# Reordering the turn of a period in layer 0: transposes ahead of the output's first tile, its evacuation behind 13 taps

## The chip, the cores and the metric

The kernel runs on one core of a Trainium2 chip. The metric is the time of the whole kernel on the device in microseconds (us), as the median of several runs; lower is better. Durations of single instructions come from one profiled execution.

## What is computed

The input x has two images of 512 channels and 64 x 64 pixels, in float32. Two layers follow, each added to its input; the change concerns the first only.

```
# layer 0: x = x + L0(group_norm(x))
xproj  = inp @ in_w + in_b                         # 512 -> 512, per pixel
x1     = gelu(layer_norm(depthwise_3x3(inp) + dw_b))
offset = x1 @ off_w + off_b                        # 16 groups x 9 points x 2
mask   = softmax((x1 @ mask_w + mask_b) over the 9 points)
out    = dcnv3(xproj, offset, mask)                # bilinear samples of xproj, weighted by the mask
L0     = out @ out_w + out_b
# layer 1: x = x + relu(batch_norm(fc(px + softmax(scores(px)) @ v(px)))) on group_norm(x)
```

## The kernel before

Layer 0 takes the first third of the time (to about 1275 us). Each image is cut into 8 chunks of 512 pixels (8 rows of 64), so there are 16 chunks. The bilinear samples of a pixel lie in a window of 5 x 5 pixels; the kernel turns offsets and mask into 25 weights for each pixel and group, and sampling becomes a matmul of a small weight matrix with a patch of xproj. The work on a chunk has four stages, each a Python generator whose `yield`s mark steps:

- `project(i)`, 13 steps: read the raw rows (`raw`, L737); four ACT instructions that normalize them to `xn` (L748); then four times a matmul `pq` (L758) and an ACT copy to `xj` (L764) with two stores to `xt` in HBM (L766).
- `features(i)`, 39 steps: four ACT instructions that seed `conv` with one tap of the depthwise kernel (L783); 32 DVE instructions for the other taps (L788), with sums `tot` on POOL (L794, L796); a matmul for the mean (L801), the subtraction (L806), squares (L809), a matmul for the variance, root (L818), reciprocal and product (L820, L821), and Gelu in two steps (L825).
- `weights(i)`, 27 steps: four times a matmul `po` (L842) and a DVE add into `o` (L847); exp, hats and softmax on ACT and DVE; nine steps with products `pk` (L885) added to `aw` (L890); one ACT copy of `aw` to `at` (L893); then four times four transposes (`p_tr`, L901) with an ACT copy to `awT` (L902).
- `sample(i)`: eight times four matmuls `pb` (L930) and a copy to `bt` (L935); eight times eight matmuls `pa` (L949) of a patch with `bt` and four copies of 32 partitions each to `dT` (L960), with reads of `res` (L941) and the fetch of the next chunk's half patch after the last of a half (`fetch`, eight DMAs, L914); then four output tiles, each a matmul `py` (L969), and in a step of its own the addition of the residual on DVE (L974), its statistics (L975) and a store `wx` (L976).

A fifth generator, `image_stats(1)`, has 64 steps; each loads one piece `xraw` of the second image (L711), two steps ahead of its use, and takes `bn_stats` of an earlier one on DVE (L713). Period 5 begins by running what is left of it, the group norm's small steps.

A loop over the 16 chunks calls `period` once for each. In it, `m` is the sampling of chunk i, `y` the rest of the sampling of chunk i - 1 (its output tiles), `v` the rest of the weights of chunk i (the transposes), `w` the weights of chunk i + 1 up to `at`, `f` the features of chunk i + 2, `g` the first step (seeds) of those of chunk i + 3, `p` the projection of chunk i + 3, and `more` a step of the statistics. `m(2)` means two steps of `m`. Chains of chunks beyond the last are empty, as is `y` in period 0.

The order of these calls is written out by hand and fixes the order of instructions on every engine and queue, since the loop runs under `tc.manual_schedule()`; each engine executes its own list in that order and waits by semaphores. All DMAs of this stage are issued from SP's queue, in the same order. PSUM has four banks under the tag "mm" (`pq`, `po`, `p_tr`, `py` and the means) and two double ones under "big" (`pb`, `pa`). `xj`, `dT` and `patch` have two buffers each, `raw` and `xraw` three, `res` four; `conv`, `at` and `aw` have one.

Of the kernel before, what the change touches and what calls it, by code (L numbers as in the profile page):

```python
# [570 lines left out]
def window_path(ctx: ExitStack, tc: tile.TileContext, t_in: dict, out: bass.AP, far: bass.AP, sums: bass.AP):  # L571
# [58 lines left out]
    with ExitStack() as l0:  # L630
# [66 lines left out]
        def image_stats(n):  # L697

            mv = sm.tile([P, KB, 2], F32, name="gn_mv")
            size = CH if n == 0 else CH // 2  # L700
            pieces, ahead = deque((kb, h) for kb in range(KB) for h in range(S // size)), deque()
            for kb in range(KB):
                st = sm.tile([P, 16, 6], F32, name="gn_st")
                for h in range(S // size):
                    if n == 0:
                        t = img[kb][:, h * size : (h + 1) * size]
                    else:
                        while len(ahead) < 3 and pieces:
                            k2, h2 = pieces.popleft()
                            ahead.append(io.tile([P, size], F32, name="xraw", bufs=3))  # L710
                            nc.sync.dma_start(ahead[-1], x_v[n, :, k2, h2 * size : (h2 + 1) * size])  # L711
                        t = ahead.popleft()
                    nc.vector.bn_stats(st[:, h, :], t)  # L713
                    yield
                nc.vector.bn_aggr(mv[:, kb, :], st[:, : S // size].rearrange("p a b -> p (a b)"))
            yield
            result = []
            yield from group_norm_steps(mv, KB, sm, ps, result)
            sc, bi = result
            gn[n] = [sm.tile([P, KB], F32, name=f"gn_{k}{n}") for k in ("scale", "bias")]  # L720
            nc.vector.tensor_copy(gn[n][0], sc)
            nc.vector.tensor_copy(gn[n][1], bi)
# [184 lines left out]
        def fetch(i, s):  # L907

            if i >= NSEQ:
                return  # L910
            n, ch = divmod(i, NCH)
            t = io.tile([P, PX, C], F32, name="patch", bufs=2)
            for p in range(PX):
                nc.sync.dma_start(  # L914
                    t[:SN, p, :], xt_d[n][ch * ROWS + PR * s : ch * ROWS + PR * s + SY, PC * p : PC * p + SX, :]
                )
            patches[i, s] = t

        def sample(i):

            n, ch = divmod(i, NCH)
            at = [awT[32 * t : 32 * t + NW].rearrange("w g (c s r p) -> w c r g s p", c=2, s=2, r=PR) for t in range(4)]

            for d0 in range(0, PR * PC, 4):
                pb = ps.tile([P, 4, 2 * PX * G], F32, tag="big", bufs=2, name="pb")

                for k in (0, 2, 1, 3):
                    r, c = divmod(d0 + k, PC)
                    off, t = SEL0 - (r * SX + c), c // 2
                    nc.tensor.matmul(  # L930
                        pb[:SN, k, :], sel[32 * t : 32 * t + NW, off : off + SN], at[t][:, c % 2, r], start=True, stop=True
                    )

                copy = nc.vector.tensor_copy if i == NSEQ - 1 and d0 % PC else nc.scalar.copy
                copy(bt[:SN].rearrange("s g q d -> s d (g q)")[:, d0 : d0 + 4, :], pb[:SN])  # L935
                yield
            res = {}

            def read(cb):
                res[cb] = io.tile([P, CH], F32, name="res", bufs=4)  # L940
                nc.sync.dma_start(res[cb], x_v[n, :, cb, ch * CH : (ch + 1) * CH])  # L941

            dT = cv.tile([P, KB, CH], F32, tag="dT", name="dT", bufs=2)
            for s in range(2):
                xp = patches.pop((i, s))
                for cb in range(KB):
                    pa = ps.tile([P, PX, 4, PR * PC], F32, tag="big", bufs=2, name="pa")
                    for p in range(PX):
                        nc.tensor.matmul(  # L949
                            pa[:, p], xp[:SN, p, cb * P : (cb + 1) * P],  # L950
                            bt[:SN, 4 * cb : 4 * cb + 4, PX * s + p, :], start=True, stop=True,
                        )

                    for q in range(4):
                        rows = slice(CG * q, CG * (q + 1))
                        dst = dT[rows, cb, s * (CH // 2) : (s + 1) * (CH // 2)].rearrange(
                            "p (r q c) -> p q r c", r=PR, c=PC)
                        src = pa[rows, :, q, :].rearrange("p q (r c) -> p q r c", c=PC)
                        copy = nc.vector.tensor_copy if i == NSEQ - 1 and q % 2 else nc.scalar.copy
                        copy(dst, src)  # L960
                    if s:
                        read(cb)
                    if cb == KB - 1:
                        fetch(i + 1, s)
                    yield
            for cb in range(KB):
                py = ps.tile([P, CH], F32, tag="mm", name="py")
                for kb in range(KB):
                    nc.tensor.matmul(  # L969
                        py, out_w[:, kb, cb * P : (cb + 1) * P], dT[:, kb, :], start=(kb == 0), stop=(kb == KB - 1)  # L970
                    )
                yield
                t = res.pop(cb)
                nc.vector.scalar_tensor_tensor(t, py, out_b[:, cb : cb + 1], t, ALU.add, ALU.add)  # L974
                nc.vector.bn_stats(stats2[n][:, cb, ch, :], t)  # L975
                nc.sync.dma_start(x1_d[n][ch][:, cb, :], t)  # L976
                yield
# [20 lines left out]
        def period(y, v, m, w, f, g, p, more):  # L998

            p()
            y()
            v(4)
            f(4)
            y()
            for taps in (9, 7, 6, 6):
                m(2)
                w()  # L1010
                more()
                f(taps)
                w()
                more()
            w()
            m()
            w()
            m()
            f()
            y()  # L1020
            f()
            m()
            p()
            w(2)
            y(2)
            w()
            m()
            p()
            f()
            w(2)  # L1030
            p()
            y(2)
            f()
            y()
            m()
            p()
            more()
            for k, steps in enumerate((1, 2, 2, 2)):
                p()
                w(steps)  # L1040
                if k == 0:
                    f()
                p()
                more()
                if k < 3:
                    m()
                if k == 0:
                    f()
                if k == 2:
                    g()  # L1050
            w()

        def value_weights():

# [26 lines left out]
        v = Chain(weights, 0)  # L1081
        v(23)
        run(features(1), project(2), output_bias())
        fetch(0, 0)
        fetch(0, 1)
        later, y, f = image_stats(1), Chain(sample, NSEQ), Chain(features, 2)
        with tc.manual_schedule():
            f()
            for i in range(NSEQ):
                if i == NCH - 3:  # L1090
                    run(later)
                w, m, g = Chain(weights, i + 1), Chain(sample, i), Chain(features, i + 3)
                period(y, v, m, w, f, g, Chain(project, i + 3), lambda: next(later, None))
                y, v, f = m, w, g
            y.rest()
# [5 lines left out]
    with ExitStack() as l1, tc.manual_schedule():  # L1101
# [8 lines left out]
        with ExitStack() as at, ExitStack() as inner:  # L1110
# [177 lines left out]
            for n in range(NB):  # L1288
# [9 lines left out]
                for i in range(NCH // 2):  # L1298
                    if 0 < i < 3 or n and i == 0:
                        k = i + 1 if i else 1  # L1300
# [26 lines left out]
                for qb in range(NCH):  # L1327
                    acc = {}
                    for kp in range(NPAIR + 2):
# [23 lines left out]
                        if kp < NPAIR:  # L1353
                            v = ready.pop(0)
                            e, tt, _ = made[qb, kp]
                            ops = operands(lambda k: e[:, k, :], tt)
                        else:
                            v = w7[:, kp - NPAIR]
# [174 lines left out]
```

## Time and profile before

| What | us |
|---|---|
| median of 3 runs (3700.46 to 3703.06) | 3702.26 |
| the profiled execution, its own time | 3707.44 |
| its span | 3705.6 |
| PE busy with matmuls | 3417.9 (92%) |
| DVE busy | 2345.8 (63%) |
| ACT busy | 1304.1 (35%) |
| POOL busy | 291.0 (8%) |
| a period from turn 1 to turn 5 | 72.9 to 75.9 |
| a period from turn 7 to turn 13 | 67.6 to 67.7 |
| period 14 | 56.9 |

The busy times of PE are modelled from pipelined matmuls, so 92% does not mean 92% of its peak. A matmul in float32 leaves two records in the trace. The shares of the page are averages over two layers with different limits; the change is confined to the periods of layer 0, whose length is the distance from one `p_tr` to the next.

In a line of the timeline the columns are start, duration, engine, line of the kernel, operation, output<-inputs, shapes and count; in brackets stand the idle time of the engine ahead of it and what ended that. In the chain of waits they are start, duration and what was at work; "SPq" is SP's queue that issues DMAs.

### The profile page before, as it was taken

The numbers are of one execution on the slowest core, as the hardware profiler recorded it, in microseconds if no ns is written. First come the engines' busy times: TensorE is split into PE (matmuls) and PEld (weight loads), VectorE is DVE, ScalarE is ACT, GpSimd is POOL, SyncE is SP. The second block draws the span as 40 slices with busy tenths as digits, with TensorE's granted clock in tenths as the row PEclk, the third lists the DMA queues.
The fourth block names the chain that finished last, engine by engine and source line by source line (L and its number), as shares of the span: only waits on it lengthen the run. The fifth ranks groups of instructions, "written<-read, shape, count | busy, mean of one in ns | idle before, by whom it ended". The sixth has DMA issues, their size and how long they took to land.

```text
span 3705.6 us, 39010 instructions
## 1 busy us (share of the span) xinstructions
PE 3417.9 (92%) x15151; PEld 2433.8 (66%) x15151; DVE 2345.8 (63%) x3575; ACT 1304.1 (35%) x1691; POOL 291.0 (8%) x190
## 2 busy tenths in 40 slices
PE   4689998999998799999999999999999999999990
PEld 1355555555555477777777777777777777777770
DVE  5798989999996475545554554567455455545544
ACT  2476777787886321111111111221111111111114
POOL 2112111212111030000000000022000000000000
PEclk9789999999999899999999999999999999999995
DMA  7233442342432444334334333444433333243349
GB/s 240 63 98 114 135 137 83 115 133 83 127 109 78 142 157 171 126 129 139 123 108 163 122 125 130 140 155 169 149 121 111 122 138 111 101 149 121 111 162 389
DMA packets 180181, 500.06 MB, mean 135 GB/s; under 512 B 22640, under 2 KB 64368, under 8 KB 170512
## 3 DMA queue, kind: packets, MB, share of 16 engines
q1 hardware_dynamic: 176496, 473.34, 37.5%
q10 hardware_dynamic: 3456, 24.12, 1.7%
q8 instruction: 121, 1.98, 0.2%
q14 instruction: 76, 0.62, 0.0%
q0 software_dynamic: 32, 0.00, 0.0%
HBM read 406.09 MB, written 91.29 MB: 134 GB/s over the span
## 4 chain that ended last, share of the span: by engine, by line
PE 75%; DVE 15%; DMA 4%; ACT 2%; SPq 1%; issue 1%; POOL 1%; ACTq 0%; DVEq 0%; POOLq 0%
PE acc L1364 41%; DVE conv L788 8%; PE pS L1211 7%; PE p L1402 7%; PE py L969 5%; PE pq L758 4%; PE pa L949 4%; PE pv L1251 3%; PE pk L1305 1%; PE p_mean L801 1%; DVE pk L885 1%; DVE aw L890 1%; DMA patch<-xt 1%; DMA out<-ct 1%; DVE o L847 1%
## 5 line engine op out<-in xcount | busy, mean ns | idle before, releaser
L1364 PE MATMUL acc<-e,v 128*128 128x256 f32 x3072 | 768.2, 386 | 0.0
L1215 ACT ACTIVATE e<-pS 128x1024 f32<-128x1024 f32 x256 | 262.0, 1024 | 1386.4 <-PE pS L1211 1313.0
L1364 PE MATMUL acc<-tt,v 128*128 128x256 f32 x3072 | 748.2, 380 | 0.5 <-DMA v<-wv 0.5
L1364 PEld LDWEIGHTS acc<-e,v 128*128 128x128 f32 x3072 | 566.5, 190 | 233.2 <-issue 165.3
L1364 PEld LDWEIGHTS acc<-tt,v 128*128 128x128 f32 x3072 | 582.4, 190 | 91.2 <-issue 10.6
L1218 DVE TENSOR_TENSOR t<-e 128x256 f32<-128x256 f32 x256 | 108.8, 425 | 761.1 <-ACT e L1215 761.1
L788 DVE SCALAR_TENSOR_TENSOR conv<-xn,L_conv_dw_w_sb,conv 128x504 f32<-128x504 f32 (+1 forms) x512 | 399.7, 795 | 48.5 <-ACT conv L783 36.5
L1228 DVE TENSOR_TENSOR tot<-tot,e 128x512 f32<-128x512 f32 x480 | 330.1, 688 | 8.3
L949 PEld LDWEIGHTS pa<-bt,patch 96*128 96x128 f32 x2048 | 251.8, 197 | 63.1 <-issue 39.4
L1211 PE MATMUL pS<-q,kq 64*128 64x512 f32 x1024 | 289.0, 641 | 0.0
L949 PE MATMUL pa<-bt,patch 96*128 96x128 f32 x2048 | 255.3, 281 | 9.3 <-ACT dT L960 5.8
L935 ACT COPY bt<-pb 96x1024 f32<-96x1024 f32 x124 | 234.2, 2001 | 58.9 <-PE pb L930 58.9
L758 PE MATMUL pq<-L_conv_in_w_sb,xn 128*128 128x512 f32 x512 | 236.3, 605 | 4.3 <-ACT xn L748 4.3
L969 PE MATMUL py<-dT,L_conv_out_w_sb 128*128 128x512 f32 x512 | 238.0, 610 | 0.0
L1402 PE MATMUL p<-t,v 128*128 128x256 f32 x1024 | 231.4, 382 | 1.7 <-DMA v<-wv 1.7
L1402 PEld LDWEIGHTS p<-t,v 128*128 128x128 f32 x1024 | 192.1, 190 | 48.5 <-issue 21.2
L960 ACT COPY dT<-pa 32x256 f32<-32x256 f32 x496 | 179.5, 362 | 89.8 <-PE pa L949 80.9
L842 PE MATMUL po<-om_w_pg,feat 128*128 128x432 f32 x512 | 203.4, 542 | 0.0
L969 PEld LDWEIGHTS py<-dT,L_conv_out_w_sb 128*128 128x128 f32 x512 | 99.3, 197 | 119.6 <-issue 115.5
L758 PEld LDWEIGHTS pq<-L_conv_in_w_sb,xn 128*128 128x128 f32 x512 | 94.1, 194 | 109.5 <-issue 93.0
L842 PEld LDWEIGHTS po<-om_w_pg,feat 128*128 128x128 f32 x512 | 93.0, 191 | 90.5 <-issue 89.4
L1211 PEld LDWEIGHTS pS<-q,kq 64*128 64x128 f32 x1024 | 77.1, 184 | 84.9 <-issue 84.9
(203 smaller groups left out, 3731.2 us busy)
## 6 DMA issues: line engine op xcount, KB each, us to landing
v<-wv SPq DMA_DIRECT2D x252, 768.0 KB
patch<-xt SPq DMA_DIRECT2D x256, 192.0 KB
v<-wv SPq DMA_DIRECT2D x256, 128.0 KB
wv<-v SPq DMA_DIRECT2D x32, 896.0 KB
xt<-xj SPq DMA_DIRECT2D x128, 128.0 KB
res<-in_x SPq DMA_DIRECT2D x64, 256.0 KB
wx<-res SPq DMA_DIRECT2D x64, 256.0 KB
xq<-wx SPq DMA_DIRECT2D x16, 1024.0 KB
```

Source lines behind the costliest of these rows:

```text
L758: nc.tensor.matmul(pq, xn[:, kb, 1 + 2 * t : 3 + 2 * t, :].rearrange("p r c -> p (r c)"), in_w[:, kb, :], start=(kb == 0), stop=(kb == KB ...
L788: nc.vector.scalar_tensor_tensor(dst, src, wt, dst, ALU.mult, ALU.add)
L842: nc.tensor.matmul(po[:, : 3 * GP], f[:, kb, t * P : (t + 1) * P], om_w[:, kb].rearrange("p a k g -> p (a k g)"), start=(kb == 0), stop=(k ...
L935: copy(bt[:SN].rearrange("s g q d -> s d (g q)")[:, d0 : d0 + 4, :], pb[:SN])
L949: nc.tensor.matmul(pa[:, p], xp[:SN, p, cb * P : (cb + 1) * P], bt[:SN, 4 * cb : 4 * cb + 4, PX * s + p, :], start=True, stop=True,)
L960: copy(dst, src)
L969: nc.tensor.matmul(py, out_w[:, kb, cb * P : (cb + 1) * P], dT[:, kb, :], start=(kb == 0), stop=(kb == KB - 1))
L1211: nc.tensor.matmul(pS[:, h, :], kq[r, 2 * (kp // 4) + h, c0 : c0 + P], qs[qb][r, :], start=True, stop=True)
L1215: nc.scalar.activation(e.rearrange("p a q -> p (a q)"), pS.rearrange("p h q -> p (h q)"), AF.Exp)
L1228: nc.vector.tensor_add(tots[qb], tots[qb], e2[:, h, :])
L1364: nc.tensor.matmul(acc[j][:, cb * HQ : (cb + 1) * HQ], v[:, j, cb * P : (cb + 1) * P], ops[j], start=(kp + cb == 0), stop=(kp + cb == NPAI ...
L1402: nc.tensor.matmul(p7[:, cb * HQ : (cb + 1) * HQ], v7[:, cb * P : (cb + 1) * P], t3, start=(k + cb == 0), stop=(k + cb == NPAIR + 2),)
```

## The change

`sample` gets one more `yield`, between the eight matmuls `pa` and their copies to `dT`, so that they can be called separately. In `period`, `m()` becomes `m(2)` where `pa` is meant, and the last copies of the half (with the read of `res` and the fetch) become the last step of the period, behind the fourth `pq`, `at` and the fourth `xj`. The call `g()` moves from behind the last `pa` to ahead of the second `xj`. `at` joins the last products in `w(3)`. At the start of the next period `v(4)` (transposes) goes ahead of `y()` (the first `py`), and the second `y()` (its residual, statistics and store) from behind four taps to behind the first `f(taps)`, so behind 13.

```diff
--- before.py
+++ after.py
@@ -950,6 +950,7 @@
                             pa[:, p], xp[:SN, p, cb * P : (cb + 1) * P],
                             bt[:SN, 4 * cb : 4 * cb + 4, PX * s + p, :], start=True, stop=True,
                         )
+                    yield
 
                     for q in range(4):
                         rows = slice(CG * q, CG * (q + 1))
@@ -1001,30 +1002,31 @@
 
 
             p()
+            v(4)
             y()
-            v(4)
             f(4)
-            y()
-            for taps in (9, 7, 6, 6):
+            for k, taps in enumerate((9, 7, 6, 6)):
                 m(2)
                 w()
                 more()
                 f(taps)
+                if k == 0:
+                    y()
                 w()
                 more()
             w()
-            m()
+            m(2)
             w()
-            m()
+            m(2)
             f()
             y()
             f()
-            m()
+            m(2)
             p()
             w(2)
             y(2)
             w()
-            m()
+            m(2)
             p()
             f()
             w(2)
@@ -1032,23 +1034,32 @@
             y(2)
             f()
             y()
+            m(2)
+            p()
+            more()
+            p()
+            w()
+            f()
+            p()
+            more()
+            m(2)
+            f()
+            p()
+            w(2)
+            g()
+            p()
+            more()
+            m(2)
+            p()
+            w(2)
+            p()
+            more()
             m()
             p()
+            w(3)
+            p()
             more()
-            for k, steps in enumerate((1, 2, 2, 2)):
-                p()
-                w(steps)
-                if k == 0:
-                    f()
-                p()
-                more()
-                if k < 3:
-                    m()
-                if k == 0:
-                    f()
-                if k == 2:
-                    g()
-            w()
+            m()
 
         def value_weights():
```

## The prediction

> **What bounds the kernel now.** I call the start of a period its turn, and number turns by the period that begins there. The transposes start turns 1 to 15 at 244.15, 319.48, 395.39, 470.11, 542.97, 619.77, 687.47, 755.18, 822.88, 890.57, 958.28, 1025.98, 1093.62, 1156.94 and 1213.85 us. Everything outside the periods is untouched, so I read only them. First the busy time of each engine in one ordinary period (turn 8 to turn 9):
>
> ```profile
> 755.18:822.88 67.70, 64.44 (x309) 38.34 (x309) 62.67 (x72) 53.77 (x72) 12.98 (x9) 1.00 0.36 112
> ```
>
> The columns are length, then PE, weight load, DVE, ACT and POOL. PE has 3.3 us free, DVE 5.0, ACT 13.9: no engine has much room, so order decides. Next the waits of DVE in that period, then the timeline of its turn:
>
> ```profile
> DVE conv L788 <- ACT conv L783: 1.8, 1, 1.8
> DVE res L974 <- PE py L969: 1.4, 1, 1.4
> ```
>
> ```profile
> 747.03 0.76 DVE L890 TENSOR_TENSOR aw<-aw,pk 128x576 f32<-128x576 f32 x1
> 748.75 2.93 ACT L783 ACTIVATE conv<-xn,L_conv_dw_b_sb,L_conv_dw_w_sb 128x512 f32<-128x512 f32 x4
> ...
> 752.19 2.93 ACT L893 COPY at<-aw 128x1600 f32<-128x1600 f32 x1
> 754.12 0.75 DVE L974 SCALAR_TENSOR_TENSOR res<-py,L_conv_out_b_sb,res 128x512 f32<-128x512 f32 x1 [1.42 <-PE py L969]
> 755.18 1.97 PE L901 MATMUL p_tr<-ident,at 128*128 128x128 f32 x16 [1.10 <-ACT at L893]
> 755.87 2.05 ACT L902 COPY awT<-p_tr 128x512 f32<-128x512 f32 x4 [0.75 <-PE p_tr L901]
> 757.98 1.14 PE L930 MATMUL pb<-awT,sel 25*96 25x256 f32 x16 [0.83 <-ACT awT L902]
> 762.28 0.60 DVE L847 TENSOR_TENSOR o<-po,om_b_pg 128x432 f32<-128x432 f32 x1
> ```
>
> The two DVE waits (the fourth tile's seeds; the output's first tile py0) are its only ones there, 3.24 us. Yet a second path ends at the same instant. ACT works through Gelus, seeds and the copy `at`; PE transposes; ACT copies awT; PE runs pb and the first po; and po ends at 762.21 (759.04 + 3.17), just ahead of DVE's first `o` add at 762.28. So removing the DVE waits alone buys nothing: that add waits for po. From it on DVE is unbroken up to the tap that starts the mean, and the period's length follows.
>
> In turns 1 to 4, the second image's statistics are read as well. There the chain of waits goes through the SP queue (turn 3):
>
> ```profile
> 389.33 0.46 SPq L941
> ...
> 394.89 6.70 DMA patch<-xt
> 401.59 0.02 issue
> 401.61 4.18 DMA xraw<-in_x
> 405.79 0.03 issue
> 405.81 0.43 DVE gn_st L713
> ```
>
> The eight patch DMAs issue from 389.89; SP holds one xraw load until the eighth patch lands; the load takes 4.18 us; DVE, which needs it before its next seven taps, stands still for 2.05 us (1.62, 2.87, 2.05 and 1.34 in turns 1 to 4).
>
> **What the Trainium skill says.** "DMA: Bandwidth & Descriptors", section "Queues, rings and completion order": on each DMA engine descriptors are consumed in ring order. So a load queued behind patches and raws lands after them; the trace agrees (4.18 us here, 2.39 for an xraw load at 234.35 with no patches ahead). "TensorE: Matmul & The Clock Gate", Part 1: idle for about 3.4 us, PE falls to half clock and needs about as long busy to return. The trace agrees: after 5.8 us idle 16 pa records took 3.78 us against 1.95. "Perfetto Trace Analysis", "Optimization Strategy": equal gaps that repeat can mean too few buffers; PE's 1.10 at the transposes is no such gap (it ends with ACT's `at`), but the change makes one, below.
>
> **The change, part by part.** No instruction is added or removed; the new yield only splits pa from its evacuation, and all but the last of the eight are still taken in pairs. Moves:
>
> (a) ACT: the seeds go from behind the last dT copies to ahead of xj1; `at` and xj3 go ahead of the last dT copies. Same work. In before, the Gelu table load starts at 735.51 and xj2's slot ends at 746.42 without a gap: 10.91. Add the seeds' slot, 2.96 (748.75 to 751.71): `at` starts 749.38 (its input was ready at 747.79) and ends 752.31, 2.81 earlier than now. Then xj3 0.48 and dT 1.51: the first awT copy starts at 754.27, ends 754.86.
>
> (b) PE: transposes at 752.37, done by 754.3. Then py0, now between them and pb. py0 needs one of the four "mm" banks. They rotate: in turn 5 the fourth transpose waited 0.53 for the first awT copy, being in its bank. With four transposes ahead, py0 is the one that gets that bank: it starts at 754.9, not 754.3. 3.45 for py0 and 0.1 to start: pb at 758.45 against 757.98; the `o` add 4.30 later, 762.75 against 762.28. **+0.4** a turn (I shade +0.47 for the 0.08 by which DVE, not po, was last). Without the bank wait it is -0.15; with the ACT copies landing later than their slots, +1.0. Both ends stay: -0.2 to +1.0. Eight ordinary turns (6 to 13): **+3.2** (-1.6 to +8).
>
> (c) DVE: res0 goes behind 13 taps. From 747.8 thirteen taps take 10.1, to 757.9; res0 waits for py0 until 758.4 and ends 759.8; the add waits until 762.75. DVE's idle moves from 3.24 in two places to some 3 us in one. Queued behind it: the remaining 19 taps, exactly what sets the end. The wx store of res0 follows later; nobody near needs it.
>
> (d) SP: res3's read and the eight patches move from ahead of xj3's two stores and an xraw load to behind them; the raws stay behind the patches. In ordinary turns, cost nothing: the patches serve pa some 35 us later, raws serve xn as late. In turns 1 to 4 it costs. By (a) in turn 3, `at` starts at 389.6, xj3 at 392.5; stores, load and read (1.14 + 0.53 + 0.46 and gaps) let the patches begin at 395.4, not 389.89; the other three turns give 6.0. In its place the load gets ahead of some things: the eighth DMA before it is now the fourth patch (in before it is the eighth patch, and that is the landing it waited for), and the store of res0 is behind it. So SP issues it at some 403.5, not 401.61. Landing: before, 1.9 MB from the first patch to 401.59, less 2 us to start, is 198 GB/s; eight patches of 192 KB then take 7.8 + 2 from 395.4, to 405.2; three raws and the load (1.09 MB at the 385 GB/s of that stretch) 2.8 and 0.7 to finish: 408.7 against 405.79. **+2.9**, and I take 3.0. Lower end 0.7 (it lands 3 us after issue), upper 5.9 (whole shift). DVE reaches this load at 404.6, so it decides. The xraw load behind xj1 comes 3 us later too, and holds DVE until 391.4 ahead of its four taps; the add is then at 403.7 and the load still decides. Four turns: **+12** (3 to 23). Turn 0 has no output before it: nothing.
>
> (e) Turn 5 (group norm's steps in between): DVE is last; its taps start 0.6 sooner, res0 is the same work: **-0.4**.
>
> (f) Turns 14 and 15 have no seeds or taps: PE waits for `at`, which waits for DVE.
>
> ```profile
> 1156.94 2.42 PE L901 MATMUL p_tr<-ident,at 128*128 128x128 f32 x16 [2.33 <-ACT at L893]
> 1160.03 2.05 PE L930 MATMUL pb<-awT,sel 25*96 25x256 f32 x16 [0.68 <-ACT awT L902]
> ```
>
> py0, now done in that idle time, goes between transposes and pb. PE is then idle 6.2 us and cold: transposes 3.7 (as at 1213.85), py0 4.3, pb at 1164.9; warm by then, pb and po save 2.4 of their cold 6.75. **+2.5** there, and at turn 15, where a warmed PE makes pb cheaper, **+1.5**. Together 4 (0 to 9).
>
> Sum: 3.2 + 12 - 0.4 + 4 = 18.8. The profiled execution took 3707.44 (span 3705.6), so 3726.2 under the profiler; it lies 5.18 above the median, which I carry over: 3702.26 + 18.8 = **3721**.
>
> **Rivals.** *Patches late in full*: every turn of 1 to 4 pays the 5.9: 3702.3 + 23.6 + 3.2 + 3.6 = 3733. For it: the chain runs through the patches. Against: the load is no longer behind the eighth. 22%. *Loads covered*: statistics turns cost 0.7 and the tail's clock makes good py0: 3702.3 + 2.8 + 3 = 3708. For it: raws and patches share engines, so landing could compress. 17%. *DVE's waits are the bound*: the 3.24 of eight turns and 5.25, 4.85, 4.03, 2.76 of turns 1 to 4 all go, 42.8: 3659. It decides if po ends before DVE's 759.8, that is if pb starts before 755.5. For it: the chain of waits in turn 8 runs py0, res0, taps. Against: awT is not written before 756.3 even with `at` 2.81 earlier. 5%, most of it for a share of the gain. Mine has 56%. *Not what it says*: 7 x 2 + 1 + 1 steps are the 16 of pa, 23 of the weights are as before; nothing is displaced. No chance given.
>
> **The numbers.** A measurement of this kernel tells about 0.2% (7.4 us) from no change. Faster 0.05, same 0.17, slower 0.78. Range: -1.6 + 3 - 0.4 + 0 gives 3703, all upper ends 3742; I cut both a little, as they don't come together: 3702 to 3738.
>
> **What would show it.** In ordinary turns: seeds and py0 waits of DVE gone, an `o` add waiting some 3 us for po; py0 waiting for awT; period 68.1. In turns 1 to 4: gn_st waiting 4 us or more for xraw, period up by 3. At 14 and 15, py0 between transposes and pb. Wrong if pb comes before 757 after the same Gelu start (735.5), or if the statistics turns keep their length.

## The result, and the profile after

| What | before | after |
|---|---|---|
| median of 4 runs each, us | 3701.48 (3700.46 to 3703.06) | 3731.8 (3730.4 to 3734.12) |
| profiled execution, its own time, us | 3707.44 | 3730.4 |
| its span, us | 3705.6 | 3728.5 |

The changed kernel is slower: ratio of after to before 1.0082 (95% interval 1.0065 to 1.0100). The prediction was 3721.0 in a range of 3702 to 3738.

I lay the executions side by side by the Gelu table load (ACT, L825), which comes once in each period, ahead of the turn; "to the load of turn 1" ends at that load, and so on. Period 14 has no Gelu left. There the mark is the table load for exp (L854), behind the four `o` adds of turn 14; turn 15 comes 33.3 us after it (before). "Layer 1" is the first ACT instruction of layer 1; from there on the kernels take 2421.8 (before) and 2421.4 us (after). The second column of numbers is a later profile of the same kernel before (experiment `e10_before_again`); why it is needed is told there.

| Stretch, us | before | before again | after | after less the two |
|---|---|---|---|---|
| to the load of turn 1 | 224.11 | 222.83 | 225.63 | +1.5, +2.8 |
| turns 1 to 5 (statistics) | 299.13 | 302.24 | 316.81 | +17.7, +14.6 |
| turns 5 to 6 | 76.86 | 75.83 | 74.61 | -2.3, -1.2 |
| turns 6 to 14 (ordinary) | 541.49 | 541.45 | 545.17 | +3.7, +3.7 |
| turn 14 to the exp load | 38.95 | 36.28 | 40.68 | +1.7, +4.4 |
| exp load to layer 1 (turn 15) | 103.29 | 101.67 | 104.16 | +0.9, +2.5 |
| layer 1 begins at | 1283.83 | 1280.30 | 1307.06 | +23.2, +26.8 |

**An ordinary turn.** First the busy time of each engine in turn 8 to turn 9 after the change (length, then PE, weight load, DVE, ACT, POOL, the clock granted to PE as a share of full speed, DMA share, GB/s), then the waits of DVE in it, then the timeline of its turn:

```profile
770.30:838.48 68.18, 64.60 (x309) 38.33 (x309) 62.82 (x72) 53.53 (x73) 13.00 (x9) 1.00 0.37 112
```

```profile
DVE o L847 <- PE po L842: 2.7, 1, 2.7
DVE res L975 <- PE py L970: 0.9, 1, 0.9
```

```profile
767.26 2.99 ACT L893 COPY at<-aw 128x1600 f32<-128x1600 f32 x1
...
770.30 1.97 PE L901 MATMUL p_tr<-ident,at 128*128 128x128 f32 x16 [1.77 <-ACT at L893]
...
772.72 3.70 PE L970 MATMUL py<-dT,L_conv_out_w_sb 128*128 128x512 f32 x8 [0.45 <-ACT awT L902]
...
776.35 1.13 PE L930 MATMUL pb<-awT,sel 25*96 25x256 f32 x16
776.46 0.75 DVE L975 SCALAR_TENSOR_TENSOR res<-py,L_conv_out_b_sb,res 128x512 f32<-128x512 f32 x1 [0.88 <-PE py L970]
...
780.62 0.61 DVE L847 TENSOR_TENSOR o<-po,om_b_pg 128x432 f32<-128x432 f32 x1 [2.68 <-PE po L842]
```

Each engine's busy time is what it was to within 0.25 us; the period is 0.48 longer. DVE's two old waits, 3.24 us, are gone, and 3.6 in two new places stand for them. The table load is at 753.40, so `at` starts 13.86 behind it, pb 22.95 and the `o` add 27.22. The order on PE is transposes, a wait of 0.45 for the first awT copy, py0, pb.

**A statistics turn.** The chain of waits in turn 3 (start, duration, what was at work), and SP's own timeline there:

```profile
410.76 0.26 DVE gn_st L713
411.02 8.36 DMA xraw<-in_x
419.38 0.02 issue
419.40 0.43 DVE gn_st L713
```

```profile
403.07 0.44 SPq L941 DMA_DIRECT2D res<-in_x  x1
403.61 5.67 SPq L914 DMA_DIRECT2D patch<-xt  x8
409.32 1.44 SPq L737 DMA_DIRECT2D raw<-in_x  x3
411.02 0.33 SPq L711 DMA_DIRECT2D xraw<-in_x  x1
```

The load is issued at 411.02, lands at 419.38, and DVE stands still for nearly all of that. The table load of this turn is at 382.66: patches start 20.9 behind it (13.6 to 14.2 in the turns of before, 19.5 to 20.9 after), the load lands 36.7 behind it (29.4 to 30.9 before; 34.3, 34.5 and 34.8 in the other turns after).

**Turn 14.** PE's timeline:

```profile
1177.53 3.68 PE L901 MATMUL p_tr<-ident,at 128*128 128x128 f32 x16 [6.15 <-ACT at L893]
1181.00 3.85 PE L970 MATMUL py<-dT,L_conv_out_w_sb 128*128 128x512 f32 x8
1184.78 1.13 PE L930 MATMUL pb<-awT,sel 25*96 25x256 f32 x16
```

PE is idle for 6.15 us where py0 used to run, and py0 then stands between the transposes and pb. From 1177 to 1179 us the granted clock was 0.50, from 1182 us on 1.00.

### The profile page after: what moved, and what is told of

It reads as the page before. It is cut to its first block, busy times and chain, and to the rows that moved or that the text cites. A ratio compares the mean times of both kernels' runs of the same rounds, so it can differ in the third digit from the quotient of the medians.

```text
span 3728.5 us, 38957 instructions
## 1 busy us (share of the span) xinstructions
PE 3417.3 (92%) x15151; PEld 2434.0 (65%) x15151; DVE 2347.9 (63%) x3575; ACT 1300.0 (35%) x1691; POOL 291.7 (8%) x190
## 4 chain that ended last, share of the span: by engine, by line
PE 77%; DVE 13%; DMA 4%; ACT 2%; issue 2%; SPq 1%; POOL 1%; ACTq 0%; DVEq 0%; POOLq 0%
PE acc L1375 41%; DVE conv L788 7%; PE pS L1222 7%; PE p L1413 7%; PE py L970 5%; PE pq L758 5%; PE pa L949 4%; PE pv L1262 3%; PE pk L1316 1%; PE po L842 1%; DMA xraw<-in_x 1%; PE p_mean L801 1%; DVE aw L890 1%; DMA out<-ct 1%; DVE pk L885 1%
```

## The experiments

The theory: ordinary turns lose through py0 on PE's path, statistics turns through SP's list, the tail through an idle PE. The rival: DVE's waits are the bound. Ratios are to the kernel before as it was measured beside each run (medians of 3702.15 to 3704.12), with the 95% interval.

### Are DVE's waits the bound?

`e2_res0_late` is the kernel before with one part of the change: res0 behind 13 taps.

```diff
-            y()
-            for taps in (9, 7, 6, 6):
+            for k, taps in enumerate((9, 7, 6, 6)):
                 ...
                 f(taps)
+                if k == 0:
+                    y()
```

> The kernel before with one part of the change alone: the first output tile's residual, statistics and store go from behind 4 taps to behind 13 taps on DVE. PE, ACT and the rest as before. If the first po ends the second path at the same instant (my reading): DVE loses its wait of 1.42 us for py0 and waits for po instead; ordinary turns change by 0.1 us at most, total 3701 (plus or minus 2). If DVE's wait for py0 is the bound: 1.4 us for each of 13 turns are saved, 3683.

Measured: 3701.31, ratio 0.9991 (0.9983 to 0.9999). DVE's waits in turn 8 to 9:

```profile
DVE conv L788 <- ACT conv L783: 1.8, 1, 1.8
DVE o L847 <- PE po L842: 1.3, 1, 1.3
```

The wait of 1.4 for py0 has become one of 1.3 for po, and the period is as long as it was (67.74 against 67.69). `e3_dve_free` takes the other wait as well, by issuing the seeds ahead of xj1 (after the `w` of k == 1); all else is as in `e2_res0_late`:

```diff
+                if k == 1:
+                    g()
                 ...
-                if k == 2:
-                    g()
```

> The kernel before with two parts: the residual behind 13 taps, and the seeds of conv ahead of xj1 on ACT. Both DVE waits of the turn go (3.24 us); PE's order and SP's order stay as before (first output tile ahead of the transposes). My reading: the add into o still waits for po; ACT loses a gap of 0.72 us, so ordinary turns are up to 0.7 us shorter (8 turns, -5), turns 1 to 4 lose some 1 to 2 us each since xj2's stores and with them the patches come 3 us later: 3702 (3696 to 3708). If the DVE waits are the bound: 3.24 and more for each turn, 3660.

Measured: 3705.99, ratio 1.0008 (1.0000 to 1.0017). In an ordinary turn the only wait left is

```profile
DVE o L847 <- PE po L842: 2.4, 1, 2.4
```

and the period falls by 0.74 to 66.95, as the transposes start 0.73 earlier behind the table load (`at` itself 0.80). So the path to the first po, and not DVE, sets the period; the rival is refuted. What I had not expected is in the statistics turns: with SP's calls in the order of before, turns 1 to 5 took 312.43, 10 to 13 more than before. Against `e2_res0_late`, which shares all but the seeds, it is 13.9 more. That told me that the seeds alone delay SP's list. The size is less sure than the direction: this profiled execution took 3713.31, 7.3 above the kernel's median.

### What do the statistics turns lose, and through what?

`e1_fetch_early` is the changed kernel with the read of `res` and the patches back ahead of the copies to `dT` (so ahead of xj3's stores):

```diff
+                    if s:
+                        read(cb)
+                    if cb == KB - 1:
+                        fetch(i + 1, s)
                     yield
                     ...
-                    if s:
-                        read(cb)
-                    if cb == KB - 1:
-                        fetch(i + 1, s)
```

> The changed kernel with one thing undone: the read of the last res tile and the eight patch DMAs go back ahead of xj3's stores and the xraw load in SP's order (they are issued in the step of the last pa matmuls, not in that of their copies). PE, ACT and DVE orders stay as changed. If the late patches in SP's order cause most of the loss (turns 1 to 4 cost some 18 us of the 23 that the profiled executions differ by): the xraw load before the seven taps lands 2 us later than in the kernel before instead of 5, turns 1 to 4 give back about 12 us, ordinary turns stay 0.45 longer than before; 3719. If the loss sits on PE, in the first output tile between transposes and pb, nothing comes back: 3731.

Measured: 3723.09, ratio 1.0049 (1.0035 to 1.0063). Turns 1 to 5 took 311.24: 5.6 less than after, where theory wanted 12. Set beside `e3_dve_free`, SP's timelines say why (us behind the table load, turns 1 to 4):

| | xj1's stores | patches | load lands |
|---|---|---|---|
| before | 9.0 | 13.6 to 14.2 | 29.4 to 30.9 |
| seeds early alone (`e3_dve_free`) and `e1_fetch_early` | 12.0 | 16.6 to 16.7 | 32.6 to 33.6 |
| after | 12.0 | 19.5 to 20.9 | 34.3 to 36.7 |

The seeds, 2.96 us of ACT ahead of xj1's copy, delay its stores by 3.0, and with them everything behind them on SP. That is half of the 6 us by which the patches are late; their new place behind xj3 is the other half. In time the seeds are the larger part: `e1_fetch_early` still loses 9.0 to 12.1 of the 14.6 to 17.7. The idle time of DVE ahead of `gn_st` for a load, between 220 and 545 us (total, times), adds up alike. In the kernel before, in `e3_dve_free` and in the changed kernel:

```profile
  DMA xraw<-in_x: 8.7, 5
```

```profile
  DMA xraw<-in_x: 28.8, 14
```

```profile
  DMA xraw<-in_x: 37.2, 8
```

They rise by more than the periods lengthen, because other waits of DVE there (for py0 and the seeds) went.

To take SP's list out of it altogether, the `xraw` loads were issued from POOL's queue, in the changed kernel (`e5_xraw_pool`) and in the kernel before (`e12_before_xraw_pool`), with this edit in both:

```diff
-    nc.sync.dma_start(ahead[-1], x_v[n, :, k2, h2 * size : (h2 + 1) * size])
+    nc.gpsimd.dma_start(ahead[-1], x_v[n, :, k2, h2 * size : (h2 + 1) * size])
```

> The changed kernel with one wait taken away: the loads of the second image's pieces (xraw) are issued from POOL's queue, not from SP's list, so that they no longer stand behind xj stores, patches and raw rows there. Nothing else moves. If the place in SP's list costs turns 1 to 4 their 18 us: gn_st no longer waits several us for xraw, and 14 to 18 us come back: 3715. If the loads are late because the 16 DMA engines are full with patches and raw rows, whoever issues: waits of gn_st stay, 3729.

> The kernel before with the xraw loads from POOL's queue and nothing else. With the changed kernel on that queue (3701) it gives the effect of the change without SP's list: 0.47 for each of 8 ordinary turns and some 7 at the tail remain, less what earlier seeds save. If the change's loss in turns 1 to 4 is all SP's list: this run is 8 to 12 us faster than the changed kernel on that queue, 3691. If the change also costs something else in turns 1 to 4: 3685 or less.

Measured: changed kernel 3701.33, ratio 0.9998 (0.9989 to 1.0006); kernel before 3690.49, ratio 0.9964 (0.9951 to 0.9977). Turns 1 to 5 take 288.53 and 288.63. DVE's waits in the changed kernel from 367 to 439 us, one period's length, hold none for `xraw`:

```profile
DVE o L847 <- PE po L842: 2.2, 1, 2.2
DVE rstd L820 <- ACT rstd L818: 1.7, 1, 1.7
```

So the two orders cost the same there once these loads are off SP's list: all that the change loses in these four turns it loses through that list. The list already cost the kernel before 10.5 to 13.6 us; the change raised that to 28.3. My expectation for `e5_xraw_pool` (3715) was too small because it counted only the change's share. What remains between the two kernels, 9.1 us up to layer 1 (1275.78 less 1266.65), is the change's other loss: turns 6 to 14 give 3.8 and the tail 7.5, less 2.1 in the rest up to turn 6.

### Is it the bank that py0 waits for?

`e7_first_awT_early` moves one step of the weights (the first four transposes and their awT copy) to the end of the period, ahead of the last copies to `dT`; to match, the loop is entered one step further on:

```diff
-            v(4)
+            v(3)
             y()
             ...
             more()
+            w()
             m()
...
-        v(23)
+        v(24)
```

> The changed kernel with the first four transposes and their copy to awT moved ahead of the last dT copies (one step of the weights taken in the period before). Then the bank that the first output tile needs is free 1.5 us sooner. If py0 waits for that bank: PE's 0.45 us wait ahead of py0 goes, pb starts 0.45 sooner, ordinary periods are 67.7 and not 68.15; total 3727, which is near what can be told apart, so the periods in the profile decide. If py0's start is set by something else (its own inputs dT, PE's list): py0 starts as late, since the last dT copies are now 0.5 later: 68.2 or more.

Measured: 3735.77, ratio 1.0088 (1.0073 to 1.0104). The turn:

```profile
780.47 0.59 ACT L902 COPY awT<-p_tr 128x512 f32<-128x512 f32 x1 [0.32 <-PE p_tr L901]
780.95 1.48 ACT L961 COPY dT<-pa 32x256 f32<-32x256 f32 x4
...
781.58 3.60 PE L970 MATMUL py<-dT,L_conv_out_w_sb 128*128 128x512 f32 x8
```

With the first awT copy early, py0 no longer waits, and the period is 67.46, 0.70 below that of the changed kernel: 0.45 is the wait. The rest is py0 itself, which starts 0.17 before the transposes' last record ends (781.58 against 781.75) and takes 3.60 instead of 3.70. PE's order is the same in both, so this confirms the bank. The kernel as a whole did not gain, though I had expected 3727: turns 6 to 14 give back 5.7, but it reaches turn 1 9.6 us later (235.19): in the prologue its first four transposes wait for `at`, and the matmul for the mean behind them on PE starts at 153.59 instead of 142.58.

### The tail, and the kernel before once more

Between the first profile of before and the other kernels that share its order there, turn 14 differed. So before was run again, unchanged (`e10_before_again`).

> The kernel before, unchanged, profiled once more. The profiled executions of before and after lie 23 us apart, the medians 28 to 30. Two runs with the PE order of before had 2.7 us less between the Gelu table load and the o add of turn 14 (22.4 against 25.16), at full clock. If the first profile of before met a slow tail by chance: turn 14 takes 22.4 here, and the time up to layer 1 is some 5 us shorter, near 1279. If not: 25.2 and 1284.

Measured: 3703.74, layer 1 begins at 1280.30. PE at turn 14:

```profile
1157.72 1.97 PE L901 MATMUL p_tr<-ident,at 128*128 128x128 f32 x16 [1.15 <-ACT at L893]
1160.52 1.14 PE L930 MATMUL pb<-awT,sel 25*96 25x256 f32 x16 [0.83 <-ACT awT L902]
```

Here pb takes 1.14; in the first profile it took 2.05, and po 4.70 against 3.17. From turn 14 to the exp load it took 36.28 here, 36.28 in `e2_res0_late`, 36.25 in `e3_dve_free`, 36.26 in `e12_before_xraw_pool` and 38.95 in the first profile: PE's longer durations at this turn belong to that one execution. `e11_tail_undone` is the changed kernel with the order of before for turns 14 and 15 alone (`period` is given the number i of its chunk for it):

```diff
+            if i >= NSEQ - 2:
+                y()
             v(4)
-            y()
+            if i < NSEQ - 2:
+                y()
...
-            m()
+            m(1 if i < NSEQ - 3 else 2)
             p()
             w(3)
             p()
             more()
-            m()
+            if i < NSEQ - 3:
+                m()
```

> The changed kernel with the order of the kernel before at turns 14 and 15 alone: the first output tile ahead of the transposes, the last dT copies in their step ahead of at. Measured against usual executions of before, the changed tail costs 4.4 us (turn 14) and 3.0 (turn 15 and after). If py0 between transposes and pb causes that: 7 us come back, 3724 to 3726. If it is the clock of PE alone (cold after a longer idle time, which chance decides): 0 to 2 us, 3730.

Measured: 3726.86, ratio 1.0061 (1.0047 to 1.0075). Turn 14 to layer 1 takes 139.10 instead of 144.84: 5.7 of the change's loss is its order in the tail, where I had expected 7.

### A version that keeps what is good

PE is idle ahead of the transposes while it waits for `at`. Something that is ready can run there: the first po of the next weights. `e4_po_first` is `e1_fetch_early` with that po issued ahead of the transposes, and py0 behind the last pb:

```diff
             p()
+            w()
             v(4)
-            y()
             f(4)
             for k, taps in enumerate((9, 7, 6, 6)):
                 m(2)
-                w()
                 more()
                 f(taps)
-                if k == 0:
+                if k < 3:
+                    w(2)
+                else:
                     y()
-                w()
+                    w()
                 more()
             w()
             m(2)
             w()
+            y()
```

> A new order built on the same reading, from the changed kernel with the patches back in their place: the first po goes ahead of the transposes on PE (it waits for nothing there, and fills the time in which PE waits for the copy at), the first output tile goes behind the last pb, where PE would wait for the last bt copies, and its residual behind the hats on DVE. If pb and the first po set the turn: DVE's add no longer waits, the period falls by about 2 to 3 us in 8 ordinary turns and the tail keeps its length of before; turns 1 to 4 about as in the run with the patches early: 3685 (3672 to 3700). If the period is bound elsewhere (ACT's bt copies or DVE's total work) by the same length, ordinary periods stay near 67.7: 3710.

Measured: 3691.28, ratio 0.9965 (0.9952 to 0.9979); an ordinary period is 64.80. The turn:

```profile
753.55 3.06 PE L842 MATMUL po<-om_w_pg,feat 128*128 128x432 f32 x8
...
760.68 0.60 DVE L847 TENSOR_TENSOR o<-po,om_b_pg 128x432 f32<-128x432 f32 x1
```

The add comes 22.10 behind the table load, against 27.22 after and 26.77 before. Two groups of matmuls moved here at once, the first po and py0, and no run takes them apart; in `e3_dve_free`, where py0 does not stand on this path either, the add came at 26.02 and the period was 66.95. But turns 1 to 5 still took 312.79. `e8_po_first_seeds_late` puts the seeds back behind the last `pa`, so that xj1's stores are early again:

> The order with the first po ahead of the transposes, with the seeds of conv put back behind the last pa, as in the kernel before. xj1 and xj2 are then copied 3 us sooner, and with their stores everything behind them in SP's list. If the earlier seeds are what makes xraw late in turns 1 to 4 where the patches are already back in place: gn_st waits about as in the kernel before, these four turns give back 10 us or more, while DVE waits some 1.6 us for seeds in every turn, which costs ordinary periods 0 to 1.6: 3684 (3676 to 3694). If the seeds' place does nothing to SP's list: 3691 to 3700.

Measured: 3677.32, ratio 0.9931 (0.9917 to 0.9945); turns 1 to 5 298.87, xj1's stores again 9.0 to 9.1 behind the table load. This is the seeds' effect on SP undone: 13.9 us in four turns, and the medians of the two kernels differ by 14.0. `e6_po_first_xraw` and `e9_both` put the `xraw` loads on POOL's queue in these two:

> The order with the first po ahead of the transposes, and the xraw loads from POOL's queue as well. In that order turns 1 to 4 still lost some 3 us each to xraw while ordinary periods were 64.8. If SP's list is their cause: turns 1 to 4 fall below those of the kernel before, 3673 (3666 to 3682). If the DMA engines are: near 3690.

> The fastest order of the runs so far in ordinary periods (first po ahead of the transposes, seeds behind the last pa: 64.62 us) with the xraw loads from POOL's queue, which took turns 1 to 4 below those of the kernel before. If the two effects add: 1.2 us less in ordinary turns than with the early seeds, turns 1 to 4 about as there: 3652 (3645 to 3660). If the late seeds hold up DVE in turns 1 to 4 once xraw no longer does: 1.6 us for each, 3658.

Measured: 3653.3, ratio 0.9866 (0.9851 to 0.9881), and 3652.94, ratio 0.9861 (0.9846 to 0.9876). The two can't be told apart, and both are 1.3 to 1.4% faster than before: turns 1 to 5 take 272.79 and 276.20, and ordinary periods 64.79 and 64.61. For `e6_po_first_xraw` I had expected 3673. Turns 1 to 5 fell by 40.0 from `e4_po_first`, where I had counted on some 18: as for `e5_xraw_pool`, I had left out what the list costs even in the order of before. Busy times in an ordinary period of `e8_po_first_seeds_late`:

```profile
743.07:807.71 64.64, 63.83 (x310) 38.40 (x308) 62.59 (x72) 53.70 (x73) 12.98 (x10) 1.00 0.38 119
```

PE has 0.8 us free of 64.64. Such a period is now nearly PE's own work, where before it had 3.3 free.

## Why the prediction was right or wrong

The direction, the order of the terms and the range held. The sum, 18.8, was 4.4 short of the first profile of before and 8.0 short of the second; most of that lies in the statistics turns (d) and the tail (f).

- **(a) ACT: right.** Predicted 13.87 from table load to `at`, measured 13.86.
- **(b) PE: right.** pb 22.95 behind the table load (predicted 22.94), the add 27.22 (27.24), and py0 waits for the first awT copy, which `e7_first_awT_early` confirmed. Eight turns cost +3.7 against +3.2.
- **(c) DVE: right.** Its waits moved in front of py0 and po and bought nothing. Taking them away alone gave nothing (`e2_res0_late`), or only what ACT's earlier `at` brings (`e3_dve_free`).
- **(d) SP: right in kind, too small: +14.6 to +17.7 against +12.** The patches began 5.9 to 6.8 later (predicted 5.5 to 6.0), and the load was issued 26.8 to 28.4 behind the table load (predicted 27.8), no longer held by the eighth patch. The term that failed is the landing of the patches. I let the eighth land 9.8 behind the issue of the first (7.8 + 2). By the semaphore updates in the trace that took 12.0 to 13.2 in turns 1 to 4 after, much as in the two profiles of before (11.5 to 14.0). The load landed 2.4 to 2.7 behind the eighth patch, where I had allowed 3.5; it comes behind the patches after all, and 5.0 later than in before on average, not 2.9. Of these 5.0, 3.7 to 4.4 a turn reached the period.

  The sum behind the 9.8 counted 1.9 MB from the issue of the first patch to the landing of the eighth in turn 3 of before. The profile has 226 GB/s for that stretch, which is 2.6 MB: other transfers moved beside the patches. The stretch of turn 3 after moves at the same rate. First before, then after:

```profile
389.89:401.59 11.70, 9.77 (x50) 5.36 (x49) 9.92 (x15) 9.72 (x11) 1.44 (x1) 1.00 0.69 226
```

```profile
403.61:416.79 13.18, 13.18 (x72) 6.60 (x71) 7.28 (x11) 8.50 (x5) 0.00 (x0) 1.00 0.76 227
```

  So taking xj3's stores and a load out from among the patches did not bring these sooner, counted from the first one's issue. That the raws, now issued directly behind the patches, took their room is likely, but no run shows it.

  The cause I gave was incomplete as well. I had seen that the load behind xj1 comes 3 us later, but not that the whole list behind it does, so that putting the patches back would return only about a third (5.6).
- **(e) Turn 5:** -1.2 to -2.3, against -0.4. Small, and not pursued.
- **(f) The tail: right in kind, +6.9 against +4.** At turn 14 I credited a warmed PE with 2.4 us saved on pb and po. That saving was measured against an execution whose pb and po were slow by chance; in the other executions with that order they take 1.14 + 3.17 there, and nothing is left to save. 2.5 + 2.4 = 4.9 would have been near the 4.4 measured. Turn 15 cost 2.5, not 1.5.
- **The offset.** I carried over the 5.18 by which the first profile lay above its median. In part it was the slow turn 14, which belongs to one execution: up to layer 1 the second profile is 3.5 shorter. Against it the change costs 26.8 up to layer 1, and the medians differ by 30.3. The 26.8 includes 2.8 ahead of turn 1, which I don't assign: the first `at` comes at 149.8 to 155.2 us in kernels whose order up to there is alike.

Of the rivals, *patches late in full* gave 3733, nearer to 3731.8 than my number. That is luck in part: its term for turns 1 to 4 was 23.6, where the profiles show 14.6 to 17.7, and its tail was 3.6, where they show 6.9. But it was right that the load still lands behind the patches. *Loads covered* is refuted by waits of 5.9 to 8.3 us for `xraw`, *DVE's waits are the bound* by `e2_res0_late` and `e3_dve_free`.

## What to carry to other kernels

When an instruction is moved ahead on one engine, follow what it pushes back on that engine into the queues: 2.96 us of seeds ahead of one copy delayed its stores, and with them every transfer behind them on the same queue. Before a wait is moved or taken away, find the other path that ends at the same instant; here the way to a shorter period was to fill PE's wait for `at` with ready work and to take py0 off that path (67.7 to 64.8 us), and not to free DVE. And take a stage's baseline from more than one execution before a few us in it are priced.

## What the hardware showed that I had not expected

- **The same loads from another queue land in time, mostly because they leave earlier.** From SP's list behind patches and raws an `xraw` load took 7.5 to 8.4 us from issue to landing; from POOL's queue, in the same stage, the median was 2.6. This is the table of DMA issues of the changed kernel with that edit, from 367 to 439 us (KB each, median us to landing):

```profile
xraw<-in_x POOLq DMA_DIRECT2D x13, 128.0 KB, 2.6
```

  The moment of issue accounts for most of it. In turn 3 SP issues the load for which DVE waits 28.4 us behind the table load. POOL issues loads as their buffers come free; the last two that DVE needs up to that point leave 18.3 and 18.8 behind the table load (at 367.31), ahead of the patches, and land by 21.6. The next leaves at 28.45, when patches and raws are on their way, and takes 6.3 (5.8 to 6.3 in turns 1 to 4). POOL's timeline, then that one load in the table of issues:

```profile
385.59 1.06 POOL L711 DMA_DIRECT2D xraw<-in_x  x2
395.77 0.54 POOL L711 DMA_DIRECT2D xraw<-in_x  x1 [9.11 <-DVE gn_st L713]
```

```profile
xraw<-in_x POOLq DMA_DIRECT2D x1, 128.0 KB, 6.3
```

  The Trainium skill, "DMA: Bandwidth & Descriptors", "SWDGE vs HWDGE vs iDMA", states that the two kinds of queue feed different internal queues of a DMA engine, which takes turns between them. 5.8 to 6.3 against 7.5 to 8.4 fits that, but the loads are not issued at the same moment, so no run here shows it. "Issuing engines are not separate DMA queues" on the same page expects of a second issuing engine only the time of a sequencer, and that to be small. Here that time, the place in SP's list, was not small: moving the loads was worth 28.3 us over four turns in the changed kernel.
- **The same matmuls met half the granted clock in one execution of six.** At turn 14, in the order of before, pb and po took 2.05 + 4.70 us in the first profile, and 1.14 + 3.17 in the five others. From turn 14 to the exp load the first was 2.7 longer. Here is pb's stretch in the first profile and in `e10_before_again`; the third figure from the end is the granted clock:

```profile
1160.03:1162.01 1.98, 1.98 (x16) 1.05 (x16) 0.00 (x0) 0.00 (x0) 0.00 (x0) 0.50 0.41 156
```

```profile
1160.52:1161.58 1.06, 1.06 (x16) 0.66 (x16) 0.00 (x0) 0.00 (x0) 0.00 (x0) 1.00 0.52 195
```

  PE had been idle for 2.33 us ahead of the transposes in the first, and for 1.15 to 1.42 in the others. The length of that idle time does not decide alone: in `e9_both` it was 2.46, and the clock stayed at 1.00 there.
